# Expert selection with tokens on partitions: one threshold search for all experts, or one per expert in steps between the matmuls

## The chip, the cores and the metric

The kernel runs on one core of a Trainium2 chip. The metric is the device time of one execution in microseconds (us); smaller is better. The engines are TensorE (PE in the profile, its weight loads PEld), VectorE (DVE), ScalarE (ACT), GpSimd (POOL) and SyncE (SP), which issues DMAs.

## The reference

Two transformer-like layers run one after the other on x of (4, 1024, 256), each part normalized and added to x. The last part is a mixture of 8 experts in which each expert chooses its tokens:

```python
xt = x.reshape(n, h)                      # n = 4096 tokens, h = 256
S = jax.nn.sigmoid(xt @ Wg).T             # (8, 4096)
G, I = jax.lax.top_k(S, k)                # k = 1024 tokens for each expert
ex = xt[I]
hid = jax.nn.gelu(einsum('ekh,ehf->ekf', ex, W1) + b1[:, None, :], approximate=False)
out = (einsum('ekf,efh->ekh', hid, W2) + b2[:, None, :]) * G[..., None]
new_x = zeros_like(xt).at[I.reshape(-1)].add(out.reshape(-1, h))
```

So the kernel needs, for each expert, the 1024 tokens with the largest scores (ties go to the earlier token), and an index list of them.

## The kernel before

The stages follow one another: gated attention and a low-rank feed-forward (L0), softmax-free attention with 16 heads (L1 attention), and the experts. In all of them the order on TensorE, VectorE and ScalarE is the order of the calls in the source; GpSimd and SyncE are ordered by a scheduler, GpSimd too by the source in the last experts.

**Gating.** While the L1 attention runs, each finished block of tokens is normalized (`token_rows`, L1183), written to `tok_d` in DRAM, transposed (`turn_gating`, L1203) and multiplied by the gate weights (`gate`, L1216). The scores lie in `logits`, 128 x 256: a partition is one of 16 segments of 256 tokens for one of 8 experts. `at_once` (L1249) does this for the last 256 tokens; nothing else is left to do beside it, and `keep_busy` (L203) fills TensorE with matmuls that nobody reads.

**Selection.** After the attention the sigmoid is taken in place (L1468 to L1471, with ACT for Exp), the scores are transposed and written into columns 256 to 263 of `tok_d` (L1486), and the threshold of all experts is found at once (L1497 to L1524): 15 rounds, each fixing two bits of the threshold. A round compares the 256 columns with three candidates (L1501, with a count per partition), lets TensorE sum the counts over the 16 segments of each expert (`pn`, L1505, a matmul with the 0/1 matrix `same_b`), and picks the best candidate (`grown`, `kept`, `tried`, L1509 to L1520). Then the tokens above the threshold and the ties that still fit are numbered by two prefix sums over 256 columns (L1548, L1552), corrected by the counts of earlier segments (`pall`, `pearly`); the numbers are transposed to tokens on partitions (`place`, L1556) and split into chunk and place in the chunk (`hi`, `lo`).

**Lists.** `List` (L1571) makes an expert's index list: `chunks` (L1577) and `places` (L1591) build 0/1 matrices on VectorE, `collect` (L1601) multiplies them on TensorE, 8 matmuls for a quarter, 32 in all, into `parts`; after the last one ScalarE copies `parts` to `listed` (L1613); `gather` (L1615) turns it into indices by one matmul with `fold` (L1616) and fetches 8 chunks of 128 tokens from `tok_d` by indirect DMA (`got`).

**Feed-forward.** `feed_forward(u)` (L1805) does unit u of 16, two for each expert, 512 tokens each: 8 groups of `ph` matmuls (L1819) with a Gelu each (L1826), then 4 groups of `py` matmuls (L1842), whose results get bias and gate on VectorE (`y`, L1859, L1860) and go to `acc_d` by an adding scatter (L1861). Between the `py` groups `turn` (L1790) transposes the next unit's tokens to `xT`. In the first unit of each expert the next expert's list is made: `chunks` and `places` on VectorE behind f = 1 to 5, all `collect` matmuls in one block between `ph` and `py`, and `gather` behind the first group of `py`. The f32 matmuls run as two passes, so the profile counts 32 `ph` and 64 `py` passes in a unit. The first list (L1874 to L1880) is made ahead of all units.

Of the kernel before, what the change touches and what calls it, by code (L numbers as in the profile page):

```python
# [18 lines left out]
P = 128  # L19
D = 256  # L20
# [51 lines left out]
def kernel(  # L72
# [130 lines left out]
    def keep_busy(bank, n):  # L203

        for _ in range(n):
            nc.tensor.matmul(
                bank, lhsT=same_b, rhs=same_b.unsqueeze(1).to_broadcast([P, 4, P]), start=True, stop=True
            )
# [18 lines left out]
    with ExitStack() as st1:  # L227
# [183 lines left out]
        def later_counts():  # L411
            r = {}

            def count_int(name, shape, pattern, per_partition, tag=None):
                n_i = const.tile(shape, I32, tag=tag or name, name=name, bufs=3 if tag else 1)
                nc.gpsimd.iota(n_i, pattern=pattern, base=0, channel_multiplier=per_partition)
                return n_i

            def count(name, shape, pattern, per_partition, dtype):
                n_i = count_int(f"{name}_i", shape, pattern, per_partition, "whole")  # L420
                r[name] = const.tile(shape, dtype, name=name)
                nc.gpsimd.tensor_copy(r[name], n_i)
# [3 lines left out]
            count("count_p", [P, P], [[1, P]], 0, BF16)  # L426
            count("count_c", [P, NC], [[1, NC]], 0, BF16)
            count("count_t", [P, SEG // P, SEGB, B], [[1, SEG // P], [SEG // P, SEGB], [KT, B]], 0, BF16)
            r["count_t"] = r["count_t"].rearrange("p k z b -> p (k z b)")
# [3 lines left out]
            r["expert_i"] = count_int("expert_i", [P, P], [[1, P]], -1, "whole")  # L433
            r["column_i"] = count_int("column_i", [P, P], [[1, P]], 0, "whole")
# [7 lines left out]
        def later_constants(r):  # L442
# [14 lines left out]

            def segment(name, n, p_i):

                row = const.tile([P, n], I32, tag="whole", name=f"{name}_row", bufs=3)  # L460
                nc.vector.tensor_scalar(row, p_i, 3, B - 1, ALU.logical_shift_right, ALU.bitwise_and)
                nc.vector.tensor_scalar(p_i, p_i, 5, None, ALU.logical_shift_right)
                n_f = const.tile([P, n], F32, name=name)
                nc.vector.scalar_tensor_tensor(n_f, row, float(SEGB), p_i, ALU.mult, ALU.add)
                return n_f

            expert_i = r["expert_i"]
            nc.vector.tensor_scalar(expert_i, expert_i, NE - 1, None, ALU.bitwise_and)

            same_b = const.tile([P, P], BF16, name="same_b")  # L470
            nc.vector.tensor_scalar(same_b, expert_i, 0.0, None, ALU.is_equal)
            earlier_b = const.tile([P, P], BF16, name="earlier_b")
            nc.vector.scalar_tensor_tensor(
                earlier_b, segment("seg_m", P, r["column_i"]), segment("seg_k", 1, r["row_i"]), same_b,
                ALU.is_gt, ALU.mult,
            )
# [8 lines left out]
            for i in range(2):  # L485
                count_i = const.tile([P, 4], BF16, name=f"counts{i}")
                nc.vector.memset(count_i, float(SEG))
                counts.append(count_i)
# [4 lines left out]
            return mb1, strip, same_b, earlier_b, bits, counts, fold  # L493
# [468 lines left out]
        for t in range(NB):  # L962
# [6 lines left out]
            elif t == 1:  # L969
                mb1, strip, same_b, earlier_b, bits, counts, fold = later_constants(whole)  # L970
# [69 lines left out]
    spare = const.tile([P, 1], F32, name="spare")  # L1040
    with ExitStack() as st3:
# [96 lines left out]
        def close(t, h, oT, tiles, at_end):  # L1138
# [77 lines left out]
            def gate():  # L1216
# [15 lines left out]
                rows = slice(32 * (z0 + us[0]), 32 * (z0 + us[-1] + 1))  # L1232
                nc.vector.tensor_tensor(logits[rows, :], logits[rows, :], pg[rows, :], ALU.add)
# [15 lines left out]
            def at_once(by_weight, back):  # L1249
# [7 lines left out]
                keep_busy(idle, 4)  # L1257
# [4 lines left out]
                keep_busy(idle, 34)  # L1262
                for i, pt in pts:
                    nc.vector.tensor_tensor(y[:, i, :], pt, h[:, i, :], ALU.add)
# [13 lines left out]
                gate()  # L1278
# [155 lines left out]
    with ExitStack() as st4:  # L1434
# [5 lines left out]
        parts = parts_ps.tile([P, P + NC], F32, name="parts")  # L1440
# [15 lines left out]

        hi = keep.tile([P, NE, NTILE], BF16, name="hi")
        lo = keep.tile([P, NE, NTILE], BF16, name="lo")  # L1460
        each = keep.tile([P, P, NTILE], BF16, name="each")
        with ExitStack() as sa:
            wk = sa.enter_context(tc.tile_pool(name="gate", bufs=2))
            w1 = sa.enter_context(tc.tile_pool(name="pick", bufs=1))
            ps = sa.enter_context(tc.tile_pool(name="gate_ps", bufs=2, space=PSUM))

            sc = w1.tile([P, SEG], F32, name="sc")
            nc.vector.tensor_scalar(sc, logits, -87.0, None, ALU.max)  # L1468
            nc.scalar.activation(sc, sc, AF.Exp, scale=-1.0)
            nc.vector.tensor_scalar(sc, sc, 1.0, None, ALU.add)  # L1470
            nc.vector.reciprocal(sc, sc)  # L1471
            idle = ps.tile([P, TB], F32, tag="idle", name="idle", bufs=1)
            keep_busy(idle, 13)

            def by_token(src, name):
                pt = ps.tile([P, SEG // P, NSEG * NE], F32, tag="tp", name=name)
                for k in range(SEG // P):
                    nc.tensor.transpose(pt[:, k, :], src[:, k * P : (k + 1) * P], ident)
                return pt

            scores_t = w1.tile([P, SEG // P, SEGB, B, NE], F32, name="scores_t")
            nc.scalar.copy(scores_t.rearrange("p k z b e -> p k (z b e)"), by_token(sc, "scoreT"))
            rows_d = tok_d.rearrange("(b z k p) d -> k z p b d", b=B, z=SEGB, p=P)
            for k in range(SEG // P):
                for z in range(SEGB):
                    nc.sync.dma_start(rows_d[k, z][:, :, D : D + NE], scores_t[:, k, z])  # L1486
            nc.scalar.copy(each, count_p.unsqueeze(2).to_broadcast([P, P, NTILE]))

            nc.scalar.activation(spare, sc[:, 0:1], AF.Gelu)

            thr = w1.tile([P, 1], F32, name="thr")
            tried = bits[:, 0, :].bitcast(F32)
            for r in range(NROUND):  # L1497
                n = counts[r % 2]
                for k in range(1, 4):
                    ge = wk.tile([P, SEG], F32, tag="ge", name="ge")  # L1500
                    nc.vector.tensor_scalar(  # L1501
                        ge, sc, tried[:, k : k + 1], None, ALU.is_ge, ALU.add, accum_out=n[:, k : k + 1]
                    )
                pn = ps.tile([P, 4], F32, tag="n", name="pn")
                nc.tensor.matmul(pn, lhsT=same_b, rhs=n, start=True, stop=True)  # L1505
                if r < NROUND - 1:

                    grown = wk.tile([P, 4, 4], F32, tag="grown", name="grown")
                    nc.vector.tensor_tensor(  # L1509
# [417 lines left out]
```

## Time and profile before

| | us |
|---|---|
| median of 3 runs (lowest, highest) | 1625.43 (1624.48, 1626.8) |
| the profiled execution's own time | 1625.33 |
| its span in the trace | 1623.5 |
| end of the last gate matmuls (L1224) | 1089.5 |
| first compare of the search (L1501) | 1093.27 |
| threshold known (L1524 ends) | 1122.95 |
| first list's `which` (L1579) | 1130.42 |
| first expert's first `ph` matmul (L1819) | 1141.76 |
| one expert of the steady stretch (`ph` to `ph`, 1202.29 to 1261.38) | 59.09 |

All times of the lower rows count from the span's start. A row of the timeline gives start, duration, engine, line, operation, tiles and shapes; what stands in square brackets is the idle time before it and who ended it. The chain that ended last is followed back from the last instruction, each step to what released it. Matmuls overlap their successors, so the starts of two passes, not their durations, tell what a pass costs.

### The profile page before, as it was taken

What the parts mean: (1) busy time and instruction counts of PE and PEld (TensorE: products, weight loads), DVE (VectorE), ACT (ScalarE), POOL (GpSimd) and SP (SyncE); (2) the same over time, 40 slices, a digit from 0 to 9 for tenths busy, and PEclk for the clock granted to TensorE, in tenths of its full rate; (3) what the DMA queues carried; (4) which work ended last, traced back from release to release, by engine and by line L of the source; (5) the groups of instructions that cost most, each with busy time, mean ns of one, the idle gap of its engine ahead of it and who ended that gap; (6) DMA issues with size and microseconds to landing.
All of it is one profiled execution on the core that took longest, in us unless ns stands there. A gap on an engine that the chain in (4) does not pass through costs nothing.

```text
span 1623.5 us, 23583 instructions
## 1 busy us (share of the span) xinstructions
PE 1562.3 (96%) x9270; PEld 797.6 (49%) x9270; DVE 904.9 (56%) x2080; ACT 647.6 (40%) x1115; POOL 402.0 (25%) x436
## 2 busy tenths in 40 slices
PE   7999999999999999999999999983999999999997
PEld 3666666666322223232323224541757667566574
DVE  5555565664657787878787787767211212222145
ACT  3344444544544545454544455641221121211233
POOL 4122232222201011111101010110424324324555
PEclk9999999999999999999999999996999999999999
DMA  8300000000000000101010100031233233233355
GB/s 205 121 1 1 1 1 1 0 1 1 1 1 1 11 31 7 34 1 40 1 40 1 36 4 27 28 129 30 57 75 70 66 75 72 66 75 88 67 146 140
DMA packets 70090, 71.22 MB, mean 44 GB/s; under 512 B 23613, under 2 KB 62938, under 8 KB 69850
## 3 DMA queue, kind: packets, MB, share of 16 engines
q1 hardware_dynamic: 56096, 47.01, 9.4%
q0 software_dynamic: 13008, 21.77, 7.4%
q8 instruction: 73, 1.20, 0.3%
q10 hardware_dynamic: 874, 0.93, 0.2%
q14 instruction: 39, 0.32, 0.1%
HBM read 41.74 MB, written 27.95 MB: 43 GB/s over the span
## 4 chain that ended last, share of the span: by engine, by line
PE 92%; DVE 3%; issue 2%; POOL 1%; ACT 1%; DMA 0%; POOLq 0%; SPq 0%; ACTq 0%; DVEq 0%
PE sc L1303 17%; PE po L1329 16%; PE ph L1819 13%; PE py L1842 13%; PE py L799 4%; PE pg L691 4%; PE pv L707 3%; PE ph L855 2%; PE po L771 2%; PE pt L1145 2%; PE pv L380 2%; PE pq L356 2%; PE pq L876 2%; PE po L775 2%; PE pk L356 2%
## 5 line engine op out<-in xcount | busy, mean ns | idle before, releaser
L1312 ACT ACTIVATE w<-sc 128x512 f32<-128x512 f32 x512 | 277.9, 594 | 218.5 <-PE sc L1303 101.7
L1317 DVE TENSOR_SCALAR w<-sc 128x1024 f32<-128x1024 f32 x240 | 293.2, 1222 | 99.2 <-PE sc L1303 71.1
L1303 PE MATMUL sc<-qT,kT 32*128 32x512 f32 (+1 forms) x2304 | 294.7, 586 | 1.5 <-ACT w L1312 0.8
L1329 PE MATMUL po<-w,vaug 128*17 128x512 f32 (+1 forms) x2304 | 276.1, 550 | 1.0 <-ACT w L1315 0.3
L1842 PE MATMUL py<-w,hid 128*128 128x256 f32 x1024 | 230.1, 380 | 0.0
L1826 ACT ACTIVATE hid<-ph,mb 128x512 f32<-128x512 f32 (+1 forms) x136 | 90.1, 662 | 344.4 <-PE ph L1819 343.7
L1819 PE MATMUL ph<-xT,w 128*128 128x512 f32 (+1 forms) x544 | 222.8, 567 | 0.7 <-DVE xT L1803 0.7
L1842 PEld LDWEIGHTS py<-w,hid 128*128 128x128 f32 x1024 | 191.1, 190 | 32.0 <-issue 7.0
L1303 PEld LDWEIGHTS sc<-qT,kT 32*128 32x128 f32 x2304 | 94.4, 183 | 173.9 <-issue 157.9
L1819 PEld LDWEIGHTS ph<-xT,w 128*128 128x128 f32 x544 | 103.2, 190 | 111.1 <-issue 107.6
L1329 PEld LDWEIGHTS po<-w,vaug 128*17 128x17 f32 x2304 | 44.8, 95 | 191.5 <-issue 157.5
L1861 POOL DMA_INDIRECT acc_d<-y,idx x56 | 88.2, 1574 | 156.1 <-issue 127.0
L1628 POOL DMA_INDIRECT got<-tok_d,idx x64 | 65.9, 1030 | 152.3 <-DVE idx L1618 135.2
L1859 DVE TENSOR_TENSOR y<-py,mb 128x256 f32<-128x256 f32 x56 | 23.4, 419 | 142.3 <-PE py L1842 135.9
L1803 DVE COPY xT<-tp 128x512 f32<-128x512 f32 (+1 forms) x34 | 22.3, 660 | 91.6 <-PE tp L1798 91.6
L1067 POOL TENSOR_TENSOR rsg<-veg,mhalf 128x1 f32<-128x1 f32 x30 | 16.7, 555 | 205.0 <-DVE veg L1066 205.0
L691 PE MATMUL pg<-nT,wh 128*128 128x512 f32 x128 | 60.8, 607 | 1.5 <-ACT nT L630 1.5
L799 PE MATMUL py<-wo,oT 128*128 128x256 f32 x256 | 61.9, 385 | 0.0
L707 PE MATMUL pv<-wh,nT 128*128 128x512 f32 x128 | 59.7, 592 | 0.0
L1618 DVE CAST idx<-parts 128x8 int32<-128x8 f32 x8 | 1.3, 167 | 101.8 <-PE parts L1616 101.8
L799 PEld LDWEIGHTS py<-wo,oT 128*128 128x128 f32 x256 | 47.3, 190 | 17.2 <-issue 9.4
L572 POOL TENSOR_TENSOR x<-x,y 128x1024 f32<-128x1024 f32 x14 | 32.9, 2351 | 73.3 <-ACT y L561 73.3
(295 smaller groups left out, 1933.3 us busy)
## 6 DMA issues: line engine op xcount, KB each, us to landing
w<-in_L_ffn_W_dram SPq DMA_DIRECT2D x16, 1024.0 KB, 5.2
x<-in_L_attn_x_dram SPq DMA_DIRECT2D x8, 512.0 KB, 4.0
acc_d<-logits SPq DMA_DIRECT2D x8, 512.0 KB, 5.1
tok_d<-hg SPq DMA_DIRECT2D x32, 128.0 KB, 1.7
x_d<-x SPq DMA_DIRECT2D x7, 512.0 KB, 2.9
back_w<-acc_d SPq DMA_DIRECT2D x6, 512.0 KB
out_dram<-x SPq DMA_DIRECT2D x20, 128.0 KB, 1.7
out_dram<-back_w POOLq DMA_DIRECT2D x4, 512.0 KB
```

What stands on the lines that cost most here:

```text
L691: nc.tensor.matmul(pg, lhsT=wh[:, c, HID + e * P : HID + (e + 1) * P], rhs=d["nT"][:, c, :], start=(c == 0), stop=(c == DC - 1),)
L707: nc.tensor.matmul(pv, lhsT=d["nT"][:, c, i * P : (i + 1) * P], rhs=wh[:, c, 0:HID], start=(c == 0), stop=(c == DC - 1),)
L799: nc.tensor.matmul(py, lhsT=d["oT"][:, e, :], rhs=wo[:, e, :], start=(e == 0), stop=(e == EC - 1))
L1303: nc.tensor.matmul(sc[:, m * n : (m + 1) * n], lhsT=row["kT"][t][rows, r, (kt + m) * P : (kt + m + 1) * P], rhs=row["qT"][rows, t, q0 : q0 ...
L1312: nc.scalar.activation(w[:, j, :], sc, AF.Relu)
L1317: nc.vector.tensor_scalar(w[:, 2:4, :], pair, 0.0, None, ALU.max)
L1329: nc.tensor.matmul(po[32 * j : 32 * j + HD + 1, weighed(halves, r)], lhsT=row["v"][:, kt + m, HQ * t + 2 * j + r, :], rhs=w[:, j, m * n : ...
L1628: return nc.gpsimd.indirect_dma_start(out=dst, out_offset=None, in_=rows[:, :], in_offset=self.at_chunk(c), bounds_check=NT - 1, oob_is_er ...
L1819: nc.tensor.matmul(ph, lhsT=w1[:, c, f * P : (f + 1) * P], rhs=xT[u][:, c, h * n : (h + 1) * n], start=(c == 0), stop=(c == DC - 1),)
L1826: nc.scalar.activation(hid[:, f, h * n : (h + 1) * n], ph, AF.Gelu, bias=mb1[:, e * FC + f : e * FC + f + 1])
L1842: nc.tensor.matmul(py, lhsT=hid[:, f, i * P : (i + 1) * P], rhs=w2[:, f, :], start=(f == 0), stop=(f == FC - 1),)
L1861: scatter = nc.gpsimd.indirect_dma_start(out=acc_d[:, :], out_offset=lists[e].at_chunk(k), in_=y, in_offset=None, bounds_check=NT - 1, oob ...
```

## The change

The scores are kept with tokens on partitions (`score_t`, 128 x 32 tiles x 8 experts, in the memory of `logits`). In `at_once` the scores known so far are transposed and go through the sigmoid beside the last normalization; only those of the last two tiles follow after the last gate matmul. Two DMAs write them to `tok_d`.

Each expert now has a search of its own over its 32 columns: `compare`, 15 `tick`s, `rank`, then the list as before; `steps` has 21 in all. The counts are summed over all partitions with a matrix of ones (`all_b`), and `rank` numbers tokens by one matmul with ones and one with a triangle (`upto_b`) and two prefix sums over 32 columns. The first expert's steps run at once; the second's first three behind its gather. All other steps are taken one at a time by `go_on_with_lists`: behind each `ph` group (in unit 0 behind every second half-group) and behind each `py` group. An expert's list is begun in the second unit of the expert two before it. `collect` is done in two steps of 16 matmuls, and `gather` follows the second at once. In unit 1 both `turn` calls come behind the third `py` group. The fillers in `at_once` go from 4 and 34 to 3 and 34; the 13, 13 and 12 in the selection and the 15 behind the first gather are replaced by 8 behind the first `rank` and 4 behind the first gather.

```diff
@@ constants
-            same_b, earlier_b (which partitions hold the same expert, an earlier segment)
+            all_b = const.tile([P, P], BF16, name="all_b")
+            nc.vector.memset(all_b, 1.0)
+            upto_b = const.tile([P, P], BF16, name="upto_b")
+            nc.vector.tensor_scalar(upto_b, r["ahead_i"], 0.0, None, ALU.is_ge)
@@ at_once
-                keep_busy(idle, 4)
+                tokens = side([P, SEG // P, P], "tokens")
+                for k in range(SEG // P):
+                    nc.tensor.transpose(tokens[:, k, :], logits[:, k * P : (k + 1) * P], ident)
+                keep_busy(idle, 3)
...
                 keep_busy(idle, 34)
+                for k in range(SEG // P):
+                    nc.vector.tensor_scalar(
+                        score_t.rearrange("p (b z k) e -> p k z b e", b=B, k=SEG // P)[:, k],
+                        tokens[:, k, :].rearrange("p (z b e) -> p z b e", b=B, e=NE),
+                        -87.0, None, ALU.max,
+                    )
+                known = score_t[:, 0 : NTILE - SEG // P]
+                nc.scalar.activation(known, known, AF.Exp, scale=-1.0)
...
                 turn_gating(tiles[0])
-                gate()
+                nc.vector.tensor_scalar(known, known, 1.0, None, ALU.add)
+                nc.vector.reciprocal(known, known)
+                score_rows = tok_d.rearrange("(j p) d -> p j d", p=P)[:, :, D : D + NE]
+                nc.sync.dma_start(score_rows[:, 0 : NTILE - SEG // P], known)
+                pg, rows = gate()
+                last_logits = wk.tile([P, SEG], F32, tag="y", name="last_logits")
+                nc.vector.tensor_copy(last_logits[rows, :], pg[rows, :])
+                tokens = side([P, SEG // P, 32], "tokens")
+                for k in range(SEG // P):
+                    nc.tensor.transpose(tokens[:, k, :], last_logits[rows, k * P : (k + 1) * P], ident[rows, rows])
+                new = score_t[:, NTILE - SEG // P : NTILE]
+                nc.vector.tensor_scalar(new, tokens[:, :, 32 - NE : 32], -87.0, None, ALU.max)
+                nc.scalar.activation(new, new, AF.Exp, scale=-1.0)
+                nc.vector.tensor_scalar(new, new, 1.0, None, ALU.add)
+                nc.vector.reciprocal(new, new)
+                nc.sync.dma_start(score_rows[:, NTILE - SEG // P : NTILE], new)
@@ class List
+            def compare(self, r):
                 for k in range(1, 4):
-                    ge = wk.tile([P, SEG], F32, tag="ge", name="ge")
+                    ge = wk.tile([P, NTILE], F32, tag="ge", name="ge")
                     nc.vector.tensor_scalar(
-                        ge, sc, tried[:, k : k + 1], None, ALU.is_ge, ALU.add, accum_out=n[:, k : k + 1]
+                        ge, self.scores, self.tried[:, k : k + 1], None, ALU.is_ge, ALU.add,
+                        accum_out=counts[r % 2][:, k : k + 1],
                     )
-                nc.tensor.matmul(pn, lhsT=same_b, rhs=n, start=True, stop=True)
+            def tick(self, r):
+                nc.tensor.matmul(pn, lhsT=all_b, rhs=counts[r % 2], start=True, stop=True)
                 if r < NROUND - 1:
...
+                    self.compare(r + 1)
                 else:
...
+                    self.kinds = wk.tile([P, 2, NTILE], BF16, tag="kinds", name="kinds")
+                    for v, op in enumerate((ALU.is_gt, ALU.is_equal)):
+                        nc.vector.tensor_scalar(self.kinds[:, v, :], self.scores, thr, None, op)
+            def rank(self):
+                for n, which in enumerate((all_b, upto_b)):
+                    nc.tensor.matmul(
+                        pre[:, n].rearrange("p v j -> p (v j)"),
+                        lhsT=which,
+                        rhs=self.kinds.rearrange("p v j -> p (v j)"),
...
+                for v in range(2):
+                    nc.vector.tensor_tensor_scan(
+                        sums[:, v, 1 : NTILE + 1], ones, pre[:, 0, v, :], 0.0, ALU.mult, ALU.add
+                    )
...
+            def steps(self):
+                return [
+                    lambda: self.compare(0),
+                    *(lambda r=r: self.tick(r) for r in range(NROUND)),
+                    self.rank,
+                    self.chunks,
+                    lambda: (self.places(0), self.places(1)),
+                    lambda: (self.places(2), self.collect(0), self.places(3), self.collect(1)),
+                    lambda: (self.collect(2), self.collect(3), self.gather()),
+                ]
@@ feed_forward
-                    if coming is not None and h == TB // n - 1:
-                        if f == 1:
-                            coming.chunks()
-                        elif 2 <= f < 6:
-                            coming.places(f - 2)
+                    if u or f % 2:
+                        go_on_with_lists(u)
-            if coming is not None:
-                for part in range(4):
-                    coming.collect(part)
...
-                if i == 0 and coming is not None:
-                    coming.gather()
-                if i in (1, 2) and u + 1 < NE * QPE:
+                if u == 1:
+                    if i == 2:
+                        for c in range(DC):
+                            turn(u + 1, c)
+                elif i in (1, 2) and u + 1 < NE * QPE:
                     turn(u + 1, i - 1)
...
+                go_on_with_lists(u)
@@ ahead of the units
+        agenda = []
+        def go_on_with_lists(u):
+            if u % QPE and not agenda and u // QPE < NE - 2:
+                agenda.extend(lists[u // QPE + 2].steps())
+            if agenda:
+                agenda.pop(0)()
         first = ps.tile([P, TB], F32, tag="mm", name="idle", bufs=3)
-        keep_busy(first, 15)
+        for step in lists[0].steps():
+            step()
+            if step == lists[0].rank:
+                keep_busy(first, 8)
+        agenda.extend(lists[1].steps())
+        for _ in range(3):
+            agenda.pop(0)()
+        keep_busy(first, 4)
```

Between the scans and the end of `rank` stand nine operations on 1, 32 or 64 columns. `pn` and the two results of `rank` (`pre`) now lie in the same PSUM tile as `parts`.

## The prediction

> **What bounds the kernel now.** I read the totals and the granted clock first, then the chain that ended last, then the stretches around the expert selection, then single instructions. TensorE (PE) is busy nearly throughout, with one hole in its clock near slice 28:
>
> ```profile
> PE 1562.3 (96%) x9270; PEld 797.6 (49%) x9270; DVE 904.9 (56%) x2080; ACT 647.6 (40%) x1115; POOL 402.0 (25%) x436
> ...
> PEclk9999999999999999999999999996999999999999
> ```
>
> The busy times by stretch, around the selection, show what the hole is (columns: us, then busy and count of PE, PEld, DVE, ACT, POOL, then clock, DMA share, GB/s):
>
> ```profile
> 1090.00:1093.30 3.30, 2.96 (x13) 1.17 (x12) 2.55 (x5) 0.42 (x1) 0.00 (x0) 1.00 0.87 282
> 1093.30:1123.00 29.70, 3.17 (x17) 1.72 (x17) 25.66 (x135) 5.36 (x4) 0.00 (x0) 0.56 0.28 76
> 1123.00:1130.40 7.40, 6.47 (x25) 2.82 (x26) 5.39 (x17) 0.66 (x1) 0.00 (x0) 0.70 0.00 0
> 1130.40:1135.50 5.10, 3.95 (x41) 1.36 (x39) 3.59 (x8) 0.27 (x1) 0.00 (x0) 1.00 0.00 0
> 1135.50:1141.80 6.30, 4.79 (x23) 1.96 (x21) 0.55 (x3) 0.00 (x0) 4.36 (x4) 1.00 0.24 64
> ```
>
> From 1093.3 to 1123.0 VectorE (DVE) works 25.7 of 29.7 us through 15 dependent rounds; TensorE has 3.2 us and clock 0.56. The whole head, 1090 to 1141.8, is latency. One round, in the timeline:
>
> ```profile
> 1121.02 0.48 DVE L1501 TENSOR_SCALAR_CACHE_REDUCE ge<-sc,tried 128x256 f32<-128x256 f32 x1
> 1121.43 0.09 DVE L1501 DVE_READ_ACCUMULATOR ge<-sc,tried 128x1 bf16 x1
> ...
> 1122.23 0.09 DVE L1501 DVE_READ_ACCUMULATOR ge<-sc,tried 128x1 bf16 x1
> ...
> 1122.37 0.19 PE L1505 MATMUL pn<-counts,same_b 128*128 128x4 bf16 x1 [1.80 <-DVE ge L1501]
> 1122.60 0.16 DVE L1523 SCALAR_TENSOR_TENSOR last<-pn,tried 128x4 f32<-128x4 f32 x1 [0.28 <-PE pn L1505]
> 1122.79 0.16 DVE L1524 TENSOR_REDUCE thr<-last 128x1 f32<-128x4 f32 x1
> ```
>
> A compare starts every 0.40 us; 0.14 after the last one's end PE counts, 0.23 later DVE goes on. Rounds follow at 1.985 us.
>
> After the head the chain is TensorE alone (start, us, what):
>
> ```profile
> 1154.97 1.94 PE ph L1819 x9
> 1156.91 1.96 PE parts L1604 x29
> 1158.86 3.65 PE py L1842 x16
> 1162.51 0.01 PE parts L1616
> 1162.52 3.56 PE py L1842 x16
> 1166.08 0.44 PE tp L1798 x4
> 1166.52 3.46 PE py L1842 x16
> ```
>
> A block of 16 `py` passes takes 3.46 us undisturbed, 3.56 behind the one small matmul L1616 (list matmul `fold`, 128x8 bf16). So whatever the change puts between these passes is paid in full, while whatever leaves the head is gained in full. The prediction is the difference of two sums.
>
> **Gains in the head.** All on the path.
> (1) Start of the first compare, now 1093.27. The last gate matmuls end as before, and a 32x256 copy takes the place of the 32x256 add at 1089.53 (0.43). The bulk of the sigmoid (add and reciprocal on 240 columns) stands between the `hg` rows (end 1087.17) and that copy: 0.28 + 1.65 (1.75 for 256) ends at 1089.1, hidden by the gate matmuls; without that cover it would cost 1.9. The two 128x128 reads of `tokens` fit in the 0.79 us that DVE idles before L1264. Then two transposes (0.60 us from DVE's end to the next reader, as L1471 to L1482), max 0.17, Exp with its hops 0.45, the memsets under it, add and 16-wide reciprocal 0.45 (L1122: 0.25): start near 1091.6. Gain **1.6**.
> (2) Rounds. 256 elements take 0.40. By the two-input operations, 0.42 for 128x256 (L1550) and 0.17 for 128x16 (L1509), an element costs about 1.04 ns, so my estimate for 32 is 0.40 - 224 x 1.04 ns = 0.167. The rest of a round, 0.785, stays. 15 x (1.985 - 1.285) = **10.5**. Bounds: 0.08 (L1538 to L1540, small independent operations) gives 14.4, 0.30 gives 4.5, 0.40 gives nothing. I take 0.167: the shapes around it (128x16: 0.17) are close.
> (3) Threshold to the first list's `which`: now 1122.95 to 1130.42, 7.5 us with two 256-wide scans, a transpose through TensorE and 25 idle-filling matmuls at half clock. New: `kinds` and two matmuls to their first reader 0.6, then nine small DVE operations (up to 64 columns) at 0.2 and two short scans at 0.22: 2.8. Gain **4.6** (at 0.15 or 0.3 each: 5.1 or 3.6).
> (4) `which` to the first `ph`, 11.3 us, stays: same lists, same gathers. The score writes (now 4096 pieces of 32 B, landing by 1103 behind the weights) have until 1114; more than 11 us cover them.
> Sum **16.7**.
>
> **Costs in the stream.** Seven lists (experts 1 to 7) now run 21 steps each between TensorE's passes.
> (5) Ticks: 15 a list, less two that run under the first gather: 103, of which 73 stand behind `ph` and 30 behind `py`. Row: L1616, the same load (128x128 bf16) and nearly the same width, costs 3.56 - 3.46 = 0.10, by the starts of the passes around it 0.112: a pass's own f32 load (0.19) can't start before the small matmul does. 103 x 0.112 = **11.5**. Bounds: 0.03 (`py` is recorded 0.03 behind L1616) and 0.22 (that and the whole f32 load bare): 3.1 to 22.7. I take L1616's, the only row with both neighbours f32.
> (6) `rank`, two matmuls of 64 columns: 7 x 0.2 = **1.4** (0.1 to 0.4).
> (7) `collect` in two blocks of 16. By the starts, 32 cost 2.15 us: 0.53 for the ways in and out, the rest at 0.227 for each four but the first; two halves cost 0.53 - 0.23 = 0.3 more. 7 x 0.3 = **2.1**.
> (8) `gather` now follows its last `collect` at once. Before, 16 `py` passes hid the copy `listed`; now TensorE waits for it, with the next passes queued behind. In the head that way took 0.5 us; less the hole that is there anyway and L1616's own cost, 0.36 more. 7 x 0.36 = **2.5**.
> (9) Waits. A step lasts 4 x 0.429 + 0.11 = 1.83 us in `ph`, 3.5 in `py`; a 32-wide round 1.29, so a tick's counts are mostly there. Not at the end of a unit: there DVE first makes `y` from the last `py` (0.73 until the next start, the rows L1859 and L1860), and the first tick of the next unit is 0.2 late; seven unit borders have ticks on both sides: 1.4. Queued behind the waiting matmul are the `ph` passes, whose PSUM readers have slack. In unit 0 a tick's DVE work also delays the second half's `xT` by 0.5. Together **1.9** (0 to 3.5).
> Sum **19.4**.
> Other moves cost nothing: DVE has 12.4 busy us in a 59.1 us expert and gains some 25; each gather waits in POOL's queue behind scatters with rows to spare (POOL busy 20.9 of 59.1); the last list's gather stays in unit 12, one 1.6 us scatter later, 50 us ahead of need. On SP the second expert's weights go out behind the score writes, some 3 us later than 1088.8, and are read 60 us on. The few constants dropped from the first stage were off the path.
>
> **Clock.** The clock was 1.00 until 1096.7, 0.50 until 1127.4, then 1.00, so TensorE went slow about 3 us after the last dense matmuls and recovered 3.4 us into the 13 at 1124.0. In the new head only 8 fillers run after the first `rank`, 4 before the gather lands and 4 behind the first transpose, where 15 and 4 were. Unknown: 0 if it stays full, 3.4 if two such stretches of the first expert run at half speed. I put **0.6**, nearest to the first, as fillers still precede the passes.
>
> The Trainium skill ("TensorE: Matmul & The Clock Gate", section "Why this matters for your kernels") warns of idle gaps over some 3 us, which put the clock back to half; the row above agrees, and by it alone the first expert would lose up to 3.4 us. The same page (section "Wait — 56ns, not 53.3ns?") gives matmul starts a floor of about 25 ns however few columns: by that the ticks would be 2.6 instead of 11.5, and the sum 5.6 us under the time before; L1616's 112 ns speaks against it, since here the next load, not the matmul, is what waits.
>
> **Sum.** -16.7 + 19.4 + 0.6 = +3.3 on the profiled execution's 1625.33 (span 1623.5 and 1.8 around it; the median shown is 1625.43, 0.1 off): **1628.6 us**. A measurement of this kernel tells about 0.2%, 3.25 us, from no change, so the forecast lies on that bound.
>
> **Rivals.**
> *Faster: the f32 load hides.* Behind a 0.429 us `ph` pass there is more room to pull a load forward than behind a 0.216 us `py` pass, where L1616 stands. If a tick costs 0.04, the stream loses 7.4: 1621.2. Faster by 0.2% from 0.05 a tick down. For: PEld is busy half the time. Against: one load waits at a time in the rows around L1616.
> *About equal: ticks near 0.08*, or rounds nearer 1.1: 1625.3.
> *Slower: the compare's fixed cost.* If 32-wide compares follow at 0.30 (each has a read of the accumulator behind it), the head gains 6.0 less, and rounds of 1.68 us add 0.4 at the seven borders: 1637.4. At 0.36 a round passes 1.83, and every one of the 73 `ph` ticks waits.
> *The clock stays low* in the first expert: 3.4 instead of 0.6: 1631.4.
> *The change doesn't shorten the head*, because the one large write of scores holds the first gather: then 5 us or more of the gain go, 1634. Landing by 1103 speaks against.
>
> **Chances.** The sum as it stands, 1626 to 1632: 0.53, of it 0.26 within 0.2% and 0.27 above. Equal: 0.15. Hidden load: 0.13. Dear compares: 0.09. Low clock: 0.06. Late scores: 0.04. So faster 0.13, same 0.41, slower 0.46. The range 1622 to 1634 leaves out the hidden load at its best and the dear compares; that holds at the ends of the bounds of (2) and (5), which are not likely to be reached together.
>
> **What would show it.** In the new profile: rounds of 1.29 us in the head and `ph` starting near 1125; a unit with ticks alone longer by 12 x 0.11; starts of f32 passes 0.11 later behind each `pn`; a wait of TensorE for `listed` near 0.4 in each list, and small ones for `ge` at unit borders only. Waits for `ge` at every step, a compare over 0.25 apart, or no delay behind `pn` would prove the sum wrong.

## The result and the profile after

The changed kernel takes **1631.22 us**, median of 7 runs (1630.93 to 1632.32); the kernel before took 1626.42 beside it (7 runs, 1624.48 to 1626.8). The ratio is 1.0033, with a 95% interval of 1.0022 to 1.0045: slower by more than 0.2%. The forecast was 1628.6 with a range of 1622 to 1634. The profiled execution took 1631.22, its span is 1629.5, so it is 6.0 above the span before. The medians are 4.8 apart: the profiled execution of the kernel before, 1625.33, lies 1.1 below its median here.

First the page's totals and its row of granted clocks:

```profile
PE 1570.5 (96%) x9347; PEld 796.2 (49%) x9347; DVE 1020.7 (63%) x3103; ACT 649.5 (40%) x1116; POOL 402.3 (25%) x435
...
PEclk9999999999999999999999999997999999999999
```

TensorE has 77 instructions more and 8 us more to do, VectorE 1023 instructions and 116 us. VectorE's share of the span rises from 56% to 63%, which by itself says nothing about the time.

The stretches around the selection, in the changed kernel (columns: us, busy and count of PE, PEld, DVE, ACT, POOL, clock, DMA share, GB/s):

```profile
1092.90:1111.00 18.10, 2.30 (x14) 1.36 (x13) 14.73 (x124) 0.00 (x0) 0.00 (x0) 0.50 0.59 150
1111.00:1116.80 5.80, 4.66 (x26) 1.66 (x27) 5.11 (x21) 0.00 (x0) 0.00 (x0) 0.50 0.00 0
1116.80:1120.20 3.40, 1.82 (x26) 0.53 (x18) 1.78 (x11) 1.55 (x2) 0.09 (x1) 1.00 0.00 0
1120.20:1126.10 5.90, 4.71 (x13) 1.77 (x12) 2.35 (x18) 0.00 (x0) 4.68 (x5) 0.50 0.28 72
```

The search now ends at 1111 (before: 1123), and the first `ph` starts at 1126.16 instead of 1141.76: **15.6 us are gained** ahead of the units. The clock falls to half twice, the second time in a stretch in which TensorE is 80% busy. A round of the first search, in the timeline:

```profile
1108.63 0.27 DVE L1503 TENSOR_SCALAR_CACHE_REDUCE ge<-logits,tried 128x32 f32<-128x32 f32 x1
...
1108.83 0.27 DVE L1503 TENSOR_SCALAR_CACHE_REDUCE ge<-logits,tried 128x32 f32<-128x32 f32 x1
...
1109.35 0.16 PE L1510 MATMUL parts<-counts,all_b 128*128 128x4 bf16 x1 [1.17 <-DVE ge L1503]
...
1109.96 0.27 DVE L1503 TENSOR_SCALAR_CACHE_REDUCE ge<-logits,tried 128x32 f32<-128x32 f32 x1
```

A compare starts every 0.19 us, though each is busy for 0.27, and rounds follow at 1.33 (1108.63 to 1109.96).

From the first `ph` to the end the changed kernel needs 503.3 us, the one before 481.7: **21.6 us are lost** there. The chain in unit 11 (start, us, what):

```profile
1472.48 3.43 PE ph L1825 x8
1475.91 0.01 PE parts L1510
1475.91 1.82 PE ph L1825 x4
1477.74 0.01 PE parts L1510
```

Eight `ph` passes without anything between take 3.43, so four take 1.715; behind a tick (L1510) four take 1.83. The tick itself shows as 0.01, its price of 0.11 stands in the passes behind it. By the starts of neighbouring passes 95 of the 103 ticks cost 0.111 or 0.112; seven wait, and one stands ahead of a transpose in unit 0 (0.06). The rows on what the tick's matmul waits for, after the first `ph`:

```profile
L1510 PE MATMUL parts<-counts,all_b x103: 164/168/168, 1128.4 to 1509.7; 128*128 128x4 bf16 x103
its engine sat idle before it (us, times) until:
  issue: 15.5, 65
  DVE ge L1503: 2.6, 7
```

`issue` stands for gaps in which nothing that the profile shows was waited for. Seven ticks wait for their counts, one at each border of two units with ticks on both sides. The border of units 1 and 2, first TensorE's rows of the timeline:

```profile
1190.57 0.10 PEld L1510 LDWEIGHTS <-all_b 128*128 128x128 bf16 x1
1190.79 0.17 PE L1510 MATMUL parts<-counts,all_b 128*128 128x4 bf16 x1
1190.79 0.30 PEld L1825 LDWEIGHTS ph<-xT,w 128*128 128x128 f32 x2
...
1193.11 0.16 PE L1510 MATMUL parts<-counts,all_b 128*128 128x4 bf16 x1 [0.34 <-DVE ge L1503]
```

and VectorE's rows of the same place:

```profile
1190.98 0.42 DVE L1861 TENSOR_TENSOR y<-py,mb 128x256 f32<-128x256 f32 x1 [0.54 <-PE parts L1510]
1191.44 0.35 DVE L1862 TENSOR_SCALAR y<-y,got 128x256 f32<-128x256 f32 x1
1191.71 0.17 DVE L1514 TENSOR_TENSOR grown<-tried,bits 128x16 int32<-128x16 int32 x1
1191.98 0.17 DVE L1521 SCALAR_TENSOR_TENSOR kept<-parts,grown 128x16 f32<-128x16 f32 x1
```

The counts `pn` are summed from 1190.79 on, but `kept`, which reads them and elsewhere follows 0.20 later, starts 1.19 later: the two operations of `y` hold VectorE until `grown` starts at 1191.71, and `kept` stands behind `grown`. By the starts of the passes the tick that waits for this round (1193.11) costs 0.61 instead of 0.11. The first rows also show that the weight load of the next f32 pass starts with the small matmul (1190.79), not ahead of it, as the prediction had read it from L1616; no run separates this from the small matmul's own load (0.10). The list's end shows its own wait:

```profile
L1623 PE MATMUL parts<-fold,listed x7: 179/180/180, 1172.1 to 1523.0; 128*128 128x8 bf16 x7
...
  ACT listed L1620: 8.8, 14
```

The 14 are seven matmuls and their seven weight loads, whose idle times the profile counts apart, so 8.8 isn't a cost. The first of the matmuls, in the timeline, shows what TensorE waits:

```profile
1172.10 0.18 PE L1623 MATMUL parts<-fold,listed 128*128 128x8 bf16 x1 [0.37 <-ACT listed L1620]
```

By the starts of the passes around them, the first block of `collect` costs 1.21, the second with its `gather` 1.67, 2.88 together; before, the one block and the later `gather` cost 2.14 + 0.11 = 2.25.

### The profile page after: what moved, and what is told of

It is laid out like the page before. It is cut to its first block, busy times and chain, and to the rows that moved or that the text cites. A ratio compares the mean times of both kernels' runs of the same rounds, so it can differ in the third digit from the quotient of the medians.

```text
span 1629.5 us, 24864 instructions
## 1 busy us (share of the span) xinstructions
PE 1570.5 (96%) x9347; PEld 796.2 (49%) x9347; DVE 1020.7 (63%) x3103; ACT 649.5 (40%) x1116; POOL 402.3 (25%) x435
## 5 line engine op out<-in xcount | busy, mean ns | idle before, releaser
L1825 PE MATMUL ph<-xT,w 128*128 128x512 f32 (+1 forms) x544 | 233.7, 581 | 1.2 <-DVE xT L1810 1.1
L1825 PEld LDWEIGHTS ph<-xT,w 128*128 128x128 f32 x544 | 97.2, 191 | 104.4 <-issue 100.0
L1503 DVE TENSOR_SCALAR_CACHE_REDUCE ge<-logits,tried 128x32 f32<-128x32 f32 x336 | 72.9, 267 | 3.9
L1521 DVE SCALAR_TENSOR_TENSOR kept<-parts,grown 128x16 f32<-128x16 f32 x112 | 19.6, 175 | 59.9 <-PE parts L1510 56.9
```

The lines of the kernel that those rows point to most:

```text
L1503: nc.vector.tensor_scalar(ge, self.scores, self.tried[:, k : k + 1], None, ALU.is_ge, ALU.add, accum_out=counts[r % 2][:, k : k + 1],)
L1825: nc.tensor.matmul(ph, lhsT=w1[:, c, f * P : (f + 1) * P], rhs=xT[u][:, c, h * n : (h + 1) * n], start=(c == 0), stop=(c == DC - 1),)
```

## Theory and rivals

The theory (T), from these two traces: 15.6 are gained ahead of the units, and 21.6 paid on TensorE: bare ticks 11.5 (103 x 0.112); seven waits at unit borders 3.7 (0.5 each above a bare tick, one 0.7); `collect` in two blocks and the wait for `listed` 4.4 (7 x 0.63); `rank` 1.0 (7 x 0.141); unit 0, where the second half's `xT` stands behind a tick's work on VectorE, 0.7; the first passes at the lower clock 0.45. Rival A: the cold clock is the loss. Rival B: ticks are nearly free, and the loss is VectorE's 116 us, which shifts its place when something else moves.

## Experiments

All times are medians of 4 to 11 runs; the kernel before took 1625.6 to 1626.3 beside them. Where no other base is named, gains are counted from 1631.22, which was taken beside 1626.42; counted against the kernel before beside each run, a gain is 0.2 to 0.8 smaller.

**The list step ahead of the `y` operations.**

```diff
+                go_on_with_lists(u)
                 gates = lists[e].got[k][:, D + e : D + e + 1]
...
-                go_on_with_lists(u)
```

> The theory T reads from the two traces: the first `ph` comes 15.6 us sooner, and the stream from there to the end takes 21.6 us longer, of which 11.5 are the bare ticks (103 x 0.112), 3.7 are the first ticks after seven unit borders (0.61 instead of 0.112, because `grown` stands behind the `y` operations of the last `py` on VectorE), 4.4 are the collect in two blocks with the gather behind the second, and 2.0 the rest. Here the list step at each `py` is put ahead of that `py`'s `y` operations. T: the seven borders go back to 0.11 each, 3.5 to 3.7 us gained, about 1627.6 against 1631.2. Rival A (the loss is the clock in the cold stretches around the first rows): nothing to gain here, 1631. Rival B (the loss is VectorE's own work, which only moves its place): what the ticks no longer wait is waited by `py` or the scatters, 1631 or slower.

1628.10 (1627.57 to 1628.64), 3.1 gained. The tick's wait rows have lost the row for `ge`; what stays is:

```profile
its engine sat idle before it (us, times) until:
  issue: 15.5, 65
```

Every first tick behind a border now costs 0.11, 3.7 less in all; one other tick costs 0.42 and a `collect` 0.2 more. Rivals A and B fall for this part.

**The gather a step later, and `collect` in one block too.**

```diff
-                    lambda: (self.collect(2), self.collect(3), self.gather()),
+                    lambda: (self.collect(2), self.collect(3)),
+                    self.gather,
```

> The gather matmul of the later lists is a step of its own, one half-group behind the second collect block, so it does not wait for `listed`. T: the second block costs 1.21 again instead of 1.67 and the gather matmul 0.11 in its own place, so 0.35 is saved seven times, 2.5 us, about 1628.8. Rival (the 0.45 more of the second block is not the wait for `listed` but the price of a seventeenth small matmul in the row): 0.1 a time at most, 1630.6 or more.

```diff
-                    lambda: (self.places(2), self.collect(0), self.places(3), self.collect(1)),
-                    lambda: (self.collect(2), self.collect(3), self.gather()),
+                    lambda: (self.places(2), self.places(3)),
+                    lambda: [self.collect(part) for part in range(4)],
+                    self.gather,
```

> All 32 collect matmuls of a later list in one step, and the gather a step later, as the kernel before has it. T: the two blocks cost 1.21 + 1.67 = 2.88 and the one with its gather 2.14 + 0.11 = 2.25, so 0.63 seven times, 4.4 us, about 1626.8. Rival (splitting is free, only the wait for `listed` counts): the same gain as with the gather alone moved, 2.5 us, 1628.8.

1629.51 (1628.43 to 1631.74), 1.7 gained, and 1627.78 (1626.90 to 1628.43), 3.4 gained. The `gather` matmul has no wait for `listed` any more in either trace. The two blocks cost 1.22 each, the one block 2.14. From the first `ph` to the end the profiled executions take 500.9 and 498.6 against 503.3, so 2.4 and 4.7 less, where T has 2.5 and 4.4. The medians give less because these two executions (1628.70 and 1627.04) were 0.8 and 0.7 faster than the medians of their kernels, while the changed kernel's was at its median. Both terms are there, and splitting has a price of its own (1.7 more gained without it), which the rival of the second text denied.

**The kernel before with 144 small matmuls added.**

```diff
+        def unread(u):
+            if 1 <= u <= 12:
+                nc.tensor.matmul(parts[:, P + NC :], lhsT=same_b, rhs=counts[0], start=True, stop=True)
```

> The kernel before with 144 added 128x4 bf16 matmuls, one behind each `ph` and each `py` of units 1 to 12, that nobody reads and that wait for nothing. T: 0.1115 each wherever they stand, 16.1 us, so 16 us above the kernel before, about 1642.5. Rival (a small bf16 matmul between two f32 passes mostly hides, at 0.03 or less): at most 4.3 us, 1630.7 or less; then the loss of the change would be in waits and not in the ticks.

1643.62 (1642.58 to 1643.94) against 1625.84, **17.8 slower**; ratio 1.0106 (1.0091 to 1.0122). By the starts, 84 of them between two `ph` passes cost 0.112 each, as the ticks do. The chain in unit 2 (start, us, what) repeats what the changed kernel's showed:

```profile
1206.50 1.82 PE ph L1823 x4
1208.32 0.01 PE parts L1807
```

What goes beyond 16.1 is a wait that the edit brought in: six of the matmuls next to `gather` waited for `idx`, since both lie in `parts` (0.59 instead of 0.22 for the pair, 2.2 in all), while the six beside a `collect` block cost nothing (0.6 less). So the price of a tick needs no wait, no VectorE and no clock. Rival B's free tick falls.

**Fillers against the cold clock.** `keep_busy` with four 128x512 matmuls behind each round of the first search, and behind the two rounds of the second that run in the wait for the first gather:

```diff
+            if step in lists[0].ticks:
+                keep_busy(first, 4)
...
-        for _ in range(3):
+        agenda.pop(0)()
+        for _ in range(2):
             agenda.pop(0)()
+            keep_busy(first, 4)
```

> The changed kernel with four unread 128x512 bf16 matmuls behind each round of the first expert's search and behind the two rounds of the second expert's that stand ahead of the first `ph`, so that TensorE is not idle for more than about 0.5 us there. T: the clock of TensorE costs little, since VectorE and the gather set the end of that stretch; what can go is the 0.45 that the first `ph` passes lose at the lower clock and 0.4 in the transposes, 0.9 at most, 1630.3 against 1631.2. Rival A (the lower clock ahead of and in the first rows is the loss): several us, 1627 or less. Rival C (fillers behind a round hold up the next round's matmul): 15 rounds x 0.2 to 0.8 lost, 1634 or more.

1633.39 (1632.08 to 1633.88), 2.2 slower. T's 0.9 was wrong: the fillers delay the search. Behind the first round, in the timeline:

```profile
1093.98 1.87 PE L206 MATMUL idle<-all_b 128*128 128x512 bf16 x4
1095.64 0.21 PE L1510 MATMUL parts<-counts,all_b 128*128 128x4 bf16 x1
```

At half clock four fillers take 1.87, longer than a round, and the next `pn` stands behind them: three rounds took 1.65 to 1.76 instead of 1.33, 1.15 in all. The rest of this execution's delay lies ahead of all that the edit touches: the gate matmuls end at 1090.82 (1089.37 in the changed kernel), and the first compare starts at 1093.21; in the other profiles of kernels that share all code ahead of it, it starts between 1091.19 and 1092.33. So the time of this run doesn't price the clock. One stretch of it does in part: from `which` to the first `ph`, with the clock at 1.00 until 1119.5, it took 11.83 instead of 12.05. The same edit without the two lines on the first search does:

> The changed kernel with two times four fillers behind the second expert's two early rounds, in the wait for the first gather, and nothing else; it prices the lower clock at the first rows alone. By the two runs with these fillers and without the ones in the first expert's search, the transposes come 0.9 later, the first `ph` 0.2 sooner and unit 0 is 0.4 shorter. T: 0.6 faster, 1630.6 against 1631.2. Rival A (the lower clock there is a large part of the loss): 1628 or less. Rival C (what the run with fillers in both places lost, 2.2 us, comes from these): 1633.

1631.04 (1630.69 to 1632.08), 0.2 gained, within the spread. The fillers behind the first transpose, in the timeline, first of the changed kernel, then of this run:

```profile
1123.51 1.91 PE L206 MATMUL idle<-all_b 128*128 128x512 bf16 x4
```

```profile
1124.38 1.03 PE L206 MATMUL idle<-all_b 128*128 128x512 bf16 x4
```

They take 1.03 instead of 1.91, so the clock is up, but the first transpose starts at 1124.27 instead of 1123.25, behind the added fillers, and the first `ph` at 1126.04 instead of 1126.16. The `ph` of unit 0 are 0.4 shorter. Rivals A and C fall: by the trace the clock in these rows is worth some tenths, which the time doesn't show.

**No search for experts 2 to 8.**

```diff
+            def first_experts(self):
+                self.hi, self.lo = lists[0].hi, lists[0].lo
...
+                if self.e:
+                    return [
+                        *(lambda: None for _ in range(NROUND + 1)),
+                        self.first_experts,
```

> Leaves out of the computation: the threshold search and the ranking of experts 2 to 8, which take the first expert's tokens (and the gates of their own); the steps from the list's making on stand where they stood, behind as many empty steps. T: the 103 ticks (11.5), the border waits (3.7), the seven rank pairs (1.0) and the second half turn of unit 0 behind VectorE (0.7) go, 16.9 in all, so about 1614.3 against 1631.2. Rival A (the clock): the head's part of the loss stays, and no more than 12 is gained, 1619 or more. Rival B (VectorE's work behind the ticks delays the evacuations as well): more than 18 gained, 1613 or less.

1614.70 (1614.42 to 1615.86), 16.5 gained where T had 16.9. The stretches of units without list work are those of the kernel before, 13.73 for `ph`. From the first `ph` to the end it takes 487.0, 5.3 more than the kernel before; 4.4 of that are `collect` and `gather`.

**Four mends together.** The first and third edits above, all fillers, and in unit 0 `f % 2 == 0` for `f % 2`, so that the last half group ahead of the second `turn` carries no tick.

> The changed kernel with the list step ahead of the `y` operations, the collect in one block with the gather a step later, the fillers behind the early rounds, and the ticks of unit 0 behind even instead of odd half groups. T, by sums of single terms: 3.7 + 4.4 + 0.9 + 0.7 = 9.7, 1621.5; by what the two mends that have been timed gave (3.1 and 3.4) 8.1, 1623.1. Either is below the kernel before (1625.8 with its chip). Rival (the terms overlap, because a mended wait is waited for at the next place): 4 or less, 1627 or more.

1623.68 (1622.79 to 1624.78); ratio to before 0.9987 (0.9978 to 0.9996). 7.5 are gained, where the single runs gave 8.1 and the sum of the terms 9.7. From the first `ph` to the end it takes 494.6, 8.7 less than the changed kernel, and the terms that lie there (3.7, 4.4, 0.7 and 0.45) make 9.2: there they nearly add up. Ahead of it this execution is 1.4 later: its first compare starts 0.8 later, and the early fillers make two rounds longer (0.6). Without the fillers in the first search:

> The run with four mends, but without the fillers behind the first expert's rounds: those between the second expert's first rounds, in the wait for the first gather, stay. By the traces these early fillers stretched rounds 3 and 4 from 1.33 to 1.51 and 1.73 us, 0.6 in all, and nothing was won there. T: 1623.0 against 1623.7, and 1622.4 if the transposes behind the gather also come sooner. Rival (the early fillers are what keeps the clock up for the first rows): the first `ph` passes go cold again, 0.4 to 0.9 slower than with them, 1624.1 to 1624.6.

1623.05 (1622.07 to 1623.73), ratio 0.9983 (0.9974 to 0.9992). That is 0.6 less, as the two longer rounds have it; but the kernel before was 0.6 lower beside this run too, so the times alone don't show that early fillers cost anything. They aren't needed.

**One matmul for several experts.** If a tick's price doesn't depend on its columns (4 so far), experts 3 to 8 can be searched together: `ge` for six experts by three two-input compares and one sum, `pn` with 24 columns, ticks behind each `ph` and `py` group from unit 1 on.

```diff
+                for k in range(3):
+                    nc.vector.tensor_tensor(
+                        ge[:, :, k, :], self.scores, tried[:, :, k : k + 1].to_broadcast([P, later, NTILE]), ALU.is_ge
+                    )
...
+                    nc.vector.tensor_reduce(counts_l[r % 2][:, :, 1:4], ge, AX.X, ALU.add)
```

> The four mends, and the thresholds of experts 3 to 8 searched together: one matmul of 24 columns a round for all six, behind fifteen pieces of units 1 and 2, so 27 ticks in the stream instead of 103; the second expert's search stays by itself in unit 0. T: TensorE pays by the piece and not by the column, 76 x 0.112 = 8.5 less than with the four mends, about 1613 to 1615; a round's VectorE chain for six experts is about 2 us (the kernel before took 1.985 for eight) against 1.83 between two groups of `ph`, so 0.2 may be waited behind eight of them, 1.6, which would make it 1615 to 1616.5. Rival (the wider round delays `ph` evacuations and `xT` copies, which stand on VectorE too): 1619 or more.

1626.65 (1626.07 to 1628.58): 3 slower than the four mends, not 8 faster. Nine ticks wait, 10.4 us:

```profile
  DVE counts_l L1671: 10.4, 9
```

The round in unit 2, DVE rows of the timeline:

```profile
1198.61 1.31 DVE L1667 TENSOR_TENSOR ge_l<-logits,tried_l 128x192 bf16<-128x192 f32 x3
1199.95 0.76 DVE L1671 TENSOR_REDUCE counts_l<-ge_l 128x18 bf16<-128x576 bf16 x1
...
1201.56 1.31 DVE L1667 TENSOR_TENSOR ge_l<-logits,tried_l 128x192 bf16<-128x192 f32 x3
```

A round is 2.95 us (1198.61 to 1201.56), not 2, and each `ph` group gives it 1.83. TensorE pays the 1.1 between at six groups, and 1.4 to 1.8 where `y` operations come in between. These waits are 11.8 by the starts of the passes, more than the 8.4 that 75 ticks less would save. The rival's number is met, but these waits of TensorE cover the loss without any held-up evacuation. A tick of 24 columns that doesn't wait costs 0.112. (The expectation says 27 ticks; the trace has 28, 15 of the six and 13 of the second expert.) The remedy is distance: two experts together in unit 0, five together with a round each 3.66 us (`fs` and `ii` name the `ph` and the `py` groups of a unit behind which a step stands).

```diff
+        pair, five = Together(1, 2), Together(*range(3, NE))
...
+        put(
+            [*fs(1, 7), *ii(1, 0, 1, 2, 3), *ii(2, 1, 2, 3), *fs(3, 0, 2, 4, 6), *ii(3, 0, 1, 2, 3)], *search(five),
+        )
```

> The mends without the fillers behind the first expert's rounds (those in the wait for the first gather stay), experts 2 and 3 searched together where the changed kernel searches expert 2, and experts 4 to 8 together, a round every second group of `ph` or every `py`, 3.66 us apart. In the run with six together the round's chain on VectorE was 2.95 us by its trace (three comparisons 1.31, their sum 0.76, the rest 0.9), and its rounds behind every group of `ph` cost 1.23 instead of 0.11; without these waits, about 12, its span of 1624.6 would be 1612.6. T: here the chain of five has 3.66 us and hides, so about 1614 as a time; if the chain of two is over the 1.83 that unit 0 gives it, by up to 0.3 twelve times, up to 1617.6. Rival (VectorE's added work holds up evacuations wherever it stands): 1620 or more.

1619.30 (1619.07 to 1622.22); ratio 0.9963 (0.9949 to 0.9977). 5 above T: three ticks still wait.

```profile
  DVE counts L1672: 3.9, 3
```

With a `rank` that waits 0.8, they cost 5.2 more than bare ones by the starts of the passes. The largest, 2.9, is behind the first `ph` group of unit 3, only 1.83 behind the tick at the border, which T had overlooked. Moved apart:

```diff
-            [*fs(1, 7), *ii(1, 0, 1, 2, 3), *ii(2, 1, 2, 3), *fs(3, 0, 2, 4, 6), *ii(3, 0, 1, 2, 3)], *search(five),
+            [*fs(1, 7), *ii(1, 0, 1, 2), *fs(2, 7), *ii(2, 1, 2, 3), *fs(3, 1, 3, 5, 7), *ii(3, 0, 1, 2, 3)], *search(five),
...
+            put([(u - 1, "i", 3) if e == 2 else (u, "f", 0)], lists[e].sort)
```

> The run with two and five together, in which four rounds still had to wait by its trace: the one behind the first `ph` group of unit 3, which comes 1.83 us behind the round at the unit's border and not 3.66 (2.8 us more than a bare tick), the one at the border of units 1 and 2 behind two `xT` copies (1.04), the rank of expert 3 behind the border's `y` operations (0.83) and one in unit 0 (0.54). Here the rounds of the five in unit 3 stand behind the odd groups, the one at the border of units 1 and 2 behind the last group of unit 2, and expert 3's sorting into greater and equal at the border of units 1 and 2. T: the first three go, 4.7 us, about 1614.6. Rival (the five's rounds cost that much wherever they stand): 1618 or more.

**1615.67** (1615.46 to 1617.85); ratio to before 0.9940 (0.9926 to 0.9953). It is 1.1 above T, and the rival's 1618 falls. One wait of 0.6 is left:

```profile
  DVE counts L1672: 0.6, 1
```

From its first `ph` to the end this kernel takes 486.9, the changed one 503.3, the one before 481.7: it pays 5.2 for the gain ahead of the units instead of 21.6. Its profiled execution, 1617.85, was the longest of the five, and in it the first `ph` starts only at 1129.16, 3.0 later than in the changed kernel. The fillers in the wait for the gather ran at half clock there (eight take 3.58), and the first transpose stood behind them, 5.36 behind the start of the first gather instead of 3.14. So in that execution these fillers cost some 2 us where they were to save some tenths; the other four, up to 2.4 shorter, weren't traced, and a run without these fillers wasn't made.

## Why the prediction was right, and where its sum failed

The direction, the size within the range and the mechanism held, though the forecast of +3.3 lay near the bound of "no change", and the profiled spans differ by 6.0: a gain of some 16 ahead of the units, and about as much and more paid between TensorE's passes. By its terms:

| step | predicted | measured |
|---|---|---|
| (1) first compare sooner | 1.6 | 1.9 |
| (2) rounds | 10.5 | 9.9 (15 x (1.985 - 1.328)) |
| (3) threshold to `which` | 4.6 | 4.6 |
| (4) `which` to first `ph`, with the clock's 0.6 | -0.6 | -0.7 |
| (5) ticks | 11.5 | 11.5 |
| (6) `rank` | 1.4 | 1.0 |
| (7), (8) `collect` and `listed` | 4.6 | 4.4 |
| (9) unit borders | 1.4 | 3.7 |
| (9) `xT` in unit 0 | 0.5 | 0.7 |
| first passes at half clock | in the 0.6 | 0.45 |

Ahead of the units 15.6 came where 16.1 was expected. The clock's 0.6 was a choice between 0 and 3.4; row (4) and the first passes lost 1.15 together, and not all of row (4) is shown to be the clock's. (2) was 0.6 too large, since compares follow at 0.19 and not at 0.167. (The text on (3) has 25 fillers at half clock; the 12 at 1128.74 take 2.75, full clock. The sum doesn't rest on it.)

(5), the largest cost and the one with the widest bounds, was met by taking the one row with the same neighbours, the 0.112 of L1616. The added 144 matmuls confirm it apart from the change. The Trainium skill ("TensorE: Matmul & The Clock Gate", section "Wait — 56ns, not 53.3ns?") has small matmuls start about 25 ns apart at least; the 144 show 0.112 between f32 passes, so that floor isn't what decides here.

The step that failed is (9). It said that the first tick of the next unit "is 0.2 late", and put 1.4 for seven borders. Measured is 0.5 each, 3.7; with `xT` (9) is 4.4, above its own bounds of 0 to 3.5. The prediction had DVE make `y` from the last `py`, 0.73, ahead of the counts, but left out that `grown`, which needs no counts, is queued behind `y` too: 0.27 from its start to that of `kept`. So `kept` comes 0.99 late (1.19 instead of 0.20 behind `pn`), and a round of 1.33 needs 2.32 where a step gives 1.83: 0.49 too much. With 0.73 and 1.29 it is the prediction's 0.2. Putting the list step ahead of `y` took these waits away (3.1 of 3.7 in the time). With 3.7 for the borders the sum is 1630.9. The smaller misses partly cancel: the head and the clock were 1.0 too good, (6) to (8) 0.6 too dear.

The rivals: a hidden f32 load was wrong by the 144; dear compares (0.30) by the 0.19; the clock that stays low by the fillers (0.2 gained). The rival that the large score write holds the first gather priced it at 5 us or more; `which` to the first `ph` took 12.05 against 11.35, so there is no room for that, and the DMA share is 0.00 from 1111.0 until the gather.

Three expectations behind it fell: early fillers were to gain 0.9 and lost 2.2, a round for six experts was to take 2 us and took 2.95, and the rounds of two and five were to hide and cost 5 more. What isn't settled is what early fillers cost beyond the longer rounds (1.15 in one trace, 0.6 in the other), and why a small matmul costs 0.112: its own load and the later load of the next pass weren't taken apart.

## What to carry to other kernels

Work taken off a serial head and spread between back-to-back f32 matmuls isn't hidden: count each piece at what a small matmul between two such passes costs (here 0.112, the same from 4 to 24 columns), and make it wide and rare instead of narrow and often. Then check, for each piece, that the other engine's chain fits the distance to the next one at the narrowest place, which is the border of two loops, where other work of that engine is queued ahead of it. Fewer, wider steps only won here (7.4 us against the four mends without early fillers, 10 against the kernel before) once that chain had the room.

## What was not expected of the hardware

A two-input compare on scores that lie 32 bytes apart takes 0.44 for 192 elements and 0.21 for 64 (1.31 and 0.62 for three), 1.8 ns an element; the one-input compare with a count took 0.40 for 256 and 0.19 for 32, 0.94 ns an element. Whether the stride, the repeated second input or the bf16 output makes the difference wasn't tried; a second input alone doesn't, since a product of 256 adjacent elements took 0.42 in the kernel before (L1553). Two small matmuls in a row between f32 passes (`rank`) cost 0.141 together, little more than one. And the clock was at half from 1120.2 to 1126.1 although TensorE was busy for 4.7 of these 5.9 us; ahead of it lay a stretch at full clock with 1.8 of 3.4 busy.
